# A four-layer kernel: the scan's C operand on VectorE, group norms by tiles, and group products placed later

## The chip, the cores and the metric

The kernel runs on one core of a Trainium2 chip. A core has engines that run side by side, each with an instruction queue of its own: TensorE (PE, matrix products, with its loading of weights shown as PEld), VectorE (DVE), ScalarE (ACT), GpSimd (POOL) and SyncE (SP, which here only issues DMAs). An engine takes its instructions in order; where one needs a result of another engine it waits on a semaphore, and all behind it in that queue waits too. DMAs are issued from the queues of SP, ScalarE and GpSimd. Matrix products land in PSUM; operands and results of the rest lie in SBUF.

The metric is device time in microseconds (us) of one execution, the median of several. A profile is one more execution, recorded by the hardware.

## The reference, cut to what matters

The input is x of (1, 1024, 64, 64), float32: 1024 channels by 4096 positions. Four layers follow, each as `x = x + f(norm(x))`, where the norm is a group norm over 32 groups of 32 channels:

```python
x = x + _L0_conv_ref(_gn(x), ...)   # layer norm and a decaying running sum along the channels
x = x + _L1_conv_ref(_gn(x), ...)   # 1024 x 1024 matrix on the channels, bias
x = x + _L2_conv_ref(_gn(x), ...)   # gated selective scan, below
x = x + _L3_conv_ref(_gn(x), ...)   # 1024 x 1024 matrix on the channels, bias
```

Layer 2, cut:

```python
xz = silu(einsum('oc,bchw->bohw', in_proj_w, x) + in_proj_b)     # 3072 x 1024
x_ssm, res, gate = split(xz, 3)
xf = silu(conv1d(x_ssm, dw_w) + dw_b)                            # along the tokens, width 3
dt, B_t, C_t = parts of einsum('oc,bcn->bon', dbc_w, xf)         # 2 heads, 8 states
# x_h, dt, B_t and C_t are put in a permuted order of the tokens, by head
h = exp(dt * A) * h + dt * B_t * x_t;  y_t = einsum(h, C_t)      # scan over 4096 tokens
# y is put back into the order of the tokens
y = y * silu(gate) + res
return silu(einsum('oc,bcn->bon', out_proj_w, y) + out_proj_b)
```

The group norm needs mean and variance of a whole group, so a layer's norm can't be finished until the layer before it has written the last position of the group's channels.

## The kernel before

**Tiles.** The 1024 channels are 8 tiles of 128 rows (`CT`), the 4096 positions are 8 blocks of 512 (`NB`), taken in pairs. Matrices: `W1` of layer 1, `WX`, `WR`, `WG` (the three thirds of the input projection: scan input, res and gate), `WO` (output projection) and `W3` of layer 3.

**Products in one step.** `W1`, `WX` and `WR` are multiplied by a Strassen-like scheme with seven products instead of eight (`multiply`, L813). For a pair of blocks the operand is cut in quarters: rows are channel tiles 0 to 3 and 4 to 7 (`KH` is 4 tiles), columns are the two blocks. `b_sets` (L773) makes the operands: `b21`, `b11`, `b22` by filling (ScalarE normalizes a tile of x, `normed`, L907 to L912), `t1` to `t4` by differences on VectorE or GpSimd. An output group `g` of two has two tiles of each row half, so group 0 writes channel tiles 0, 1, 4, 5 and group 1 writes 2, 3, 6, 7. A product is 8 calls of matmul with 512 columns (L828; the hardware runs each as two passes): for each of two output tiles `o`, the four tiles `k`. Its weights, 512 KB, come by a DMA on SP's queue. Results are added on VectorE (`put` and `add`). `run` (L867) goes over pairs and matrices, yields after every product, and (with `fine`) also after its first half.

**Order.** Instructions of VectorE, TensorE, GpSimd and ScalarE run in the order in which the program is written (`tc.manual_schedule`); SP's queue is ordered by the framework. Beside the products other work is dealt out: `sort_on` works on the ranking that gives the permutation, and `sum_weights` and `sum_weights2` make sums of weight blocks on GpSimd (L457 and after) and store them for later products.

**Norms.** While a layer's result is added up, VectorE takes statistics for every tile and block (`take_stats`, L148). `moments` (L176) aggregates them to mean and variance for each of the 8 tiles (L180), and `norm_steps` (L186) brings them to groups: a matmul over the group `pg` (L194), differences `d` (L197 to L199), a second matmul `pv` (L203), `v` (L211), Ln and Exp on ScalarE (L168, L169), a refinement (L171 to L173), and the bias (L214). Layer 2's norm is made in one piece (`norm2 = group_norm("gn2")`, L959) between the last product of layer 1 and the first of `WX`.

**The scan.** It runs beside the products of `WR`. Its 74 steps take 56 tokens of each of 2 heads. `gather` (L1212) fetches permuted rows, `turn_rows` (L1226, L1227) transposes them on TensorE into PSUM (`pr`), and `spread_decay` (L1230) makes from that the operands of the next step: `cts` and `bts` are copies of C and B (L1234, L1235), GpSimd makes `cd` from `cts` (L1236: C times an 8 by 8 identity, spread to 16 x 512), and VectorE makes `D` (L1239, L1241) and spreads it over the states into `E` (L1243). `cross` multiplies `bts` and `cd` on TensorE (`pg`, L1250); `weigh` on VectorE multiplies E by pg (L1258), reduces (L1260) and writes `G` (L1263); `apply` is the product `py` of G and the gathered rows (L1267). In one turn k of the loop: turn rows k+1, weigh k-1, spread k+1, products of `WR`, apply k-1, cross k. Results of `WR` go by `put2b` and `add2b` (L976, L980) into `rg`, and `activate` (L983) applies Silu (L986) and stores four tiles to DRAM (`res_d`) on SP's queue (L988). After the last step a loop (`while silus`, L1320) stores what is left.

**Products in two steps.** `WG`, `WO` and `W3` are multiplied with the scheme applied twice (`two_steps`, L1350): outer products P1 to P7, each of seven inner ones; a product "P7P3" is inner P3 of outer P7. A pair of blocks and a matrix make a job: first a gate job and an out job in turn for each pair, then last jobs (layer 3). Each inner product has a slot, and work is put at slots (`at`, `then`, `plan`): `fetch` (L1379) loads quarters of x (1 MB each) on ScalarE's queue, `fill` (L1386) normalizes them, `inner_sum` (L1384) makes differences on GpSimd, and `emit` (L1578) adds results out of PSUM, the first by ScalarE's copy (`qZ`, `qQ`, L1589). A row half of layer 3's norm is made by `next_norm` (L1429) during the last products of the out jobs: it begins at slot 44 or 56 of the job, goes on at +2, +2, +3, +3, and ends at +4.

Of the kernel before, what the change touches and what calls it, by code (L numbers as in the profile page):

```python
# [45 lines left out]
OG = 2  # L46
# [44 lines left out]
def tile_net(ctx: ExitStack, tc: tile.TileContext, x, par_d, cst_d, w_d, w2_d, dbcw_d, out):  # L91
# [84 lines left out]
    def moments(name, ct0=0, n=CT):  # L176

        mv = small.tile([P, 2, CT], F32, tag="gn_mv", name=f"{name}_mv")
        for ct in range(n):
            nc.vector.bn_aggr(mv[:, :, ct], stats[:, ct0 + ct].rearrange("p a b -> p (a b)"))  # L180
        return mv[:, 0, :n], mv[:, 1, :n]

    def group_norm(name):
        return finish_of(norm_steps(name, *moments(name)))
# [310 lines left out]
    with tc.issue_after(exp_ln.ins), tc.tile_pool(name="l0x", bufs=2) as lx, \  # L495
# [46 lines left out]
        def norm_chunk(c):  # L542

            at = slice(c * CH, (c + 1) * CH)
            mean, var = moments(f"gn0_{c}", c * CH, CH)
            nc.vector.tensor_copy(mean0[:, at], mean)
            nc.vector.tensor_scalar_mul(nmean0[:, at], mean, -1.0)
            norms[c] = yield from norm_steps(f"gn0_{c}", mean, var, CH, layernorm=True)
# [224 lines left out]
    def b_sets(B, make, first=False, eng=None):  # L773

        def plain(name, row, col):
            B[name] = []
            for k in range(KH):
# [35 lines left out]
    def multiply(m, B, put, add, fine=False):  # L813


        for g in range(NG):
# [7 lines left out]
            def product(to, i, name, fresh):  # L824
                w = weights(m, g, i)
                for o in range(OG):
                    for k in range(KH):
                        nc.tensor.matmul(to[o], w[:, k, o * P : (o + 1) * P], B[name][k],  # L828
                                         start=(fresh and k == 0), stop=(k == KH - 1),
                                         skip_group_check=True)  # L830
                    if fine and o == 0:
                        yield True
# [34 lines left out]
    def run(pairs, mats, make, put, add, before=None, after=None, last_eng=None, fine=False, tell=False, B=None):  # L867
# [3 lines left out]
        def sets(i):  # L871
            B = {"name": f"{mats[0]}_{pairs[i]}"}
# [9 lines left out]
        if B is None:  # L882
            B, steps = sets(0)
            for _ in range(5):
                next(steps)
        else:
            steps = iter(())
        for i, pair in enumerate(pairs):
# [3 lines left out]
            for m in mats:  # L892
                for half in multiply(m, B, lambda o, c, ps: put(m, o, 2 * pair + c, ps),
                                     lambda o, c, ps: add(m, o, 2 * pair + c, ps), fine):
                    if half:
                        yield True
                        continue
# [9 lines left out]
    def normed(norm):  # L907
        scale, bias = norm

        def make(t, ct, nb, eng=[0]):  # L910
            sc, bi = scale[:, ct : ct + 1], bias[:, ct : ct + 1]
            nc.scalar.activation(t, X[nb][:, ct, :], AF.Identity, bias=bi, scale=sc)  # L912
# [3 lines left out]
    def pointwise(name, m, bias_name, order, src, dst):  # L916
        norm = finish_of(norm_steps(f"gn{name}", mean1, var1))
# [31 lines left out]
    coming[0] = next(order)  # L949
    sums = (busy for f in (sum_weights(WR, sum1, nc.scalar, lag=(1, 1)),  # L950
                               sum_weights2(WG, sum1, nc.scalar, lag=(1, 1))) for busy in f)
    with tc.manual_schedule(engines={E_.DVE, E_.PE, E_.Pool, E_.Activation}):
        for i, _ in enumerate(pointwise("l1", W1, "b1", [3, 2] + EARLY, x0_d, x1_d)):
            busy = next(sums, None) if i % 14 < 13 else None
            sort_on(not busy, (0, 0, 0, 0, 3, 2, 1, 2, 1, 3, 3, 3, 0, 0)[i % 14])
        for _ in sums:
            pass
    sum_pool.__exit__(None, None, None)


    norm2 = group_norm("gn2")
# [21 lines left out]
    def activate(n):  # L983
# [3 lines left out]
        for o, nb, r in silus[:n]:  # L987
            nc.sync.dma_start(res_d[o * P : (o + 1) * P, nb * FB : (nb + 1) * FB], r)  # L988
        del silus[:n]

    with tc.tile_pool(name="l2a", bufs=2) as pa, tc.tile_pool(name="l2a2", bufs=1) as pa2, \
# [158 lines left out]
        with tc.manual_schedule(engines={E_.DVE, E_.PE, E_.Pool, E_.Activation}):  # L1150
# [4 lines left out]
            for half in run(EARLY + LATE, [WX], normed(norm2), put2a, add2a, before2,  # L1155
                            last_eng=nc.vector, fine=True, tell=True):
# [41 lines left out]
    with tc.tile_pool(name="l2r2", bufs=8) as prg, tc.tile_pool(name="l2g", bufs=5) as pgat, tc.tile_pool(name="l2b", bufs=2) as pb, tc.tile_pool(name="l2h", bufs=1) as ph, \  # L1198
# [31 lines left out]
        def spread_decay(k, R, BC, D):  # L1230

            bts, cd = B2[k % 2]
            cts = pb.tile([HS, LC], F32, tag="cts", name=f"cts{k}")
            nc.vector.tensor_copy(cts, BC[64 + 2 * HS : 64 + 3 * HS, P:])  # L1234
            nc.vector.tensor_copy(bts[:HS], BC[64 : 64 + HS, :P])  # L1235
            nc.gpsimd.tensor_tensor(cd[:HS], cts.unsqueeze(1).to_broadcast([HS, S, LC]),  # L1236
                                    eye8.unsqueeze(2).to_broadcast([HS, S, LC]), ALU.mult)
# [6 lines left out]
                                    negA.unsqueeze(2).to_broadcast([P, S, LC]), ALU.mult)  # L1244

# [41 lines left out]
        with tc.manual_schedule(engines={E_.DVE, E_.PE, E_.Pool, E_.Activation}):  # L1287
# [32 lines left out]
            while silus:  # L1320
                activate(4)
# [27 lines left out]
    def two_steps(jobs, norm2):  # L1349
# [5 lines left out]
        scale, bias = norm2  # L1355
# [390 lines left out]
```

## Time and profile before

| | us |
|---|---|
| median of 3 executions | 2760.11 (2759.61 to 2762.84) |
| profiled execution | 2760.86 |
| span of the profile in it | 2759.0 |
| TensorE busy | 2619.3 |
| VectorE busy | 1777.6 |
| ScalarE busy | 1090.0 |
| GpSimd busy | 1303.5 |

The span is what the profile covers, from the first instruction to the last; 1.86 us of the profiled execution lie around it. Busy times overlap. The mean clock granted to TensorE was 0.980 of full speed.

The program goes through these stretches, with TensorE's busy time in each as the profile's windows give it:

| stretch, us | TensorE busy | what runs |
|---|---|---|
| 0 to 300 | 221.72 | layer 0, start of layer 1 |
| 300 to 800 | 492.91 | layer 1 (to 615), then WX |
| 800 to 1400 | 584.28 | WX and convolution, then WR with the scan |
| 1400 to 1860 | 446.56 | WR with the scan (to 1673), then the gate and out jobs |
| 1860 to 2400 | 528.09 | gate and out jobs |
| 2400 to 2759 | 345.75 | layer 3 |

In lines of the timeline the columns are the start in us, the duration in us, the engine, the line, the operation, output and inputs by the program's names, shapes, how many instructions are taken together, and in brackets how long the engine had been idle and what it waited for. `SPq`, `ACTq` and `POOLq` are DMA issues and waits in an engine's queue. In a list of waits the columns are the time waited in all, how often, and the longest.

### The profile page before, as it was taken

The numbers are of one execution on the slowest core, as the hardware profiler recorded it, in microseconds if no ns is written. First come the engines' busy times: TensorE is split into PE (matmuls) and PEld (weight loads), VectorE is DVE, ScalarE is ACT, GpSimd is POOL, SyncE is SP. The second block draws the span as 40 slices with busy tenths as digits, with TensorE's granted clock in tenths as the row PEclk, the third lists the DMA queues.
The fourth block names the chain that finished last, engine by engine and source line by source line (L and its number), as shares of the span: only waits on it lengthen the run. The fifth ranks groups of instructions, "written<-read, shape, count | busy, mean of one in ns | idle before, by whom it ended". The sixth has DMA issues, their size and how long they took to land.

```text
span 2759.0 us, 31019 instructions
## 1 busy us (share of the span) xinstructions
PE 2619.3 (95%) x9590; PEld 1728.2 (63%) x9590; DVE 1777.6 (64%) x3785; ACT 1090.0 (40%) x1838; POOL 1303.5 (47%) x1175
## 2 busy tenths in 40 slices
PE   4788999999999999999999999999999999899998
PEld 4664444444555555444444446888888888788887
DVE  7996766464454564456666565567676675777776
ACT  4783110104655654565657554322333233221220
POOL 4154324411213002467686864556566575554543
PEclk9898999999999999999999999999999999999999
DMA  7345467745533534677777875889899898788896
GB/s 283 120 163 182 164 215 251 232 130 182 166 110 99 155 112 110 187 236 223 208 200 224 240 207 176 239 246 301 218 274 280 243 298 236 246 280 304 293 332 211
DMA packets 423578, 591.47 MB, mean 214 GB/s; under 512 B 149973, under 2 KB 211541, under 8 KB 420342
## 3 DMA queue, kind: packets, MB, share of 16 engines
q1 hardware_dynamic: 297110, 362.09, 42.2%
q10 hardware_dynamic: 93568, 140.52, 14.5%
q0 software_dynamic: 32736, 86.88, 12.2%
q8 instruction: 78, 1.28, 0.2%
q14 instruction: 86, 0.70, 0.1%
HBM read 432.02 MB, written 157.36 MB: 214 GB/s over the span
## 4 chain that ended last, share of the span: by engine, by line
PE 50%; DMA 3%; POOL 3%; DVE 3%; issue 1%; ACT 1%; DVEq 0%; POOLq 0%; ACTq 0%
PE mm L828 10%; PE q_P7P L1620 5%; PE q_P5P L1620 5%; PE q_P3P L1620 5%; PE q_P6P L1620 5%; PE q_P4P L1620 5%; PE q_P1P L1620 4%; PE q_P2P L1620 4%; PE pg L1250 2%; PE py L1267 2%; DMA qD<-x_d 2%; DMA g<-tok_d,src 1%; POOL s L457 1%; PE pr L1226 1%; POOL t L786 0%
## 5 line engine op out<-in xcount | busy, mean ns | idle before, releaser
L828 PE MATMUL mm<-t,w 128*128 128x512 f32 x1536 | 686.1, 598 | 0.3 <-DVE image L926 0.3
L828 PE MATMUL mm<-b,w 128*128 128x512 f32 x1152 | 518.4, 602 | 4.8 <-ACT b L912 4.8
L828 PEld LDWEIGHTS mm<-t,w 128*128 128x128 f32 x1536 | 287.6, 191 | 329.2 <-issue 324.1
L828 PEld LDWEIGHTS mm<-b,w 128*128 128x128 f32 x1152 | 218.0, 193 | 257.6 <-issue 246.8
L1017 DVE SCALAR_TENSOR_TENSOR cvp<-xs,par,cvp 128x512 f32<-128x512 f32 x128 | 95.4, 754 | 84.2 <-ACT cvp L1014 81.9
L1044 POOL TENSOR_TENSOR acc<-l2xt,acc 128x136 f32<-128x136 f32 x56 | 27.9, 498 | 246.6 <-ACT l2xt L1038 243.3
L1589 ACT COPY qQ<-q_P5P 128x512 f32<-128x512 f32 x48 | 28.1, 586 | 287.8 <-PE q_P5P L1620 256.0
L1388 ACT ACTIVATE qb<-x_x_b,gn_bias,gn_r_r 128x512 f32<-128x512 f32 x128 | 97.1, 805 | 112.6 <-DVE qQ L1550 49.2
L457 POOL TENSOR_TENSOR s<-s 128x256 f32<-128x256 f32 (+3 forms) x120 | 128.9, 1081 | 7.8
L1276 POOL DMA_INDIRECT y_d<-y,dst x74 | 75.4, 1019 | 118.0 <-ACT y L1272 55.5
L1270 ACT COPY g<-py 8x512 f32<-8x512 f32 x146 | 83.8, 574 | 108.9 <-PE py L1267 105.4
L1258 DVE TENSOR_TENSOR E<-E,pg 128x512 f32<-128x512 f32 x74 | 50.8, 686 | 109.9 <-PE pg L1250 101.9
L786 POOL TENSOR_TENSOR t<-b,t 128x512 f32<-128x512 f32 x72 | 94.4, 1339 | 55.1 <-DVE t L786 54.9
L926 DVE SCALAR_TENSOR_TENSOR image<-mm,par,image 128x512 f32<-128x512 f32 x64 | 47.2, 746 | 107.1 <-PE mm L828 107.1
L1068 DVE TENSOR_TENSOR xs<-mm,xs 128x512 f32<-128x512 f32 x64 | 41.7, 684 | 114.7 <-PE mm L828 114.7
L1036 PEld LDWEIGHTS l2pt<-both,cv 128*128 128x128 f32 x512 | 76.6, 190 | 35.6 <-issue 25.6
L1620 PE MATMUL q_P1P<-t_b,wq_P1P 128*128 128x256 f32 x384 | 93.6, 388 | 3.5 <-issue 3.5
L1384 POOL TENSOR_TENSOR t_t<-qt 128x512 f32<-128x512 f32 x23 | 29.7, 1289 | 139.8 <-DVE qt L1384 80.3
L1384 POOL TENSOR_TENSOR t_t<-qt,t_t 128x512 f32<-128x512 f32 x46 | 69.8, 1518 | 51.3 <-DVE qt L1384 51.0
L1620 PE MATMUL q_P4P<-t_t,wq_P4P 128*128 128x256 f32 x384 | 91.1, 380 | 0.0
L912 ACT ACTIVATE b<-image,gnl_bias,gnl_r_r 128x512 f32<-128x512 f32 x48 | 36.8, 808 | 137.4 <-DMA s<-in_w_dram 58.5
L1620 PE MATMUL q_P5P<-t_t,wq_P5P 128*128 128x256 f32 x384 | 90.8, 379 | 0.0
(381 smaller groups left out, 5999.6 us busy)
## 6 DMA issues: line engine op xcount, KB each, us to landing
w<-s_d SPq DMA_DIRECT2D x96, 512.0 KB
w<-in_w_dram SPq DMA_DIRECT2D x72, 512.0 KB
x_x_b<-x_d ACTq DMA_DIRECT2D x32, 1024.0 KB
image<-x_d SPq DMA_DIRECT2D x12, 2048.0 KB
wq_P6P<-s_d SPq DMA_DIRECT2D x84, 256.0 KB
wq_P7P<-s_d SPq DMA_DIRECT2D x84, 256.0 KB
wq_P5P<-s_d SPq DMA_DIRECT2D x84, 256.0 KB
wq_P3P<-s_d SPq DMA_DIRECT2D x84, 256.0 KB
```

What stands on the lines that cost most here:

```text
L457: eng.tensor_tensor(out, a, b, ALU.subtract)
L786: eng.tensor_tensor(B[name][k], B[one][k], B[two][k], ALU.subtract)
L828: nc.tensor.matmul(to[o], w[:, k, o * P : (o + 1) * P], B[name][k], start=(fresh and k == 0), stop=(k == KH - 1), skip_group_check=True)
L1017: nc.vector.scalar_tensor_tensor(cv, xo[:, at + t : at + t + FB], pcol("dww", 3 * o + t), cv, ALU.mult, ALU.add)
L1036: nc.tensor.matmul(pt[:, q * NV : (q + 1) * NV], cv[:, (q0 + q) * P : (q0 + q + 1) * P], both[:, o, :], start=True, stop=True)
L1250: nc.tensor.matmul(pg, bts, cd.rearrange("p s t -> p (s t)"), start=True, stop=True)
L1267: nc.tensor.matmul(py, G2[k % 2], rows.pop(k)[:, :DH], start=True, stop=True)
L1270: nc.scalar.copy(rows[k + 1][h * LC : h * LC + S, :DH], py[h * LC : h * LC + S])
L1276: nc.gpsimd.indirect_dma_start(out=y_d[:, :], out_offset=bass.IndirectOffsetOnAxis(ap=dst_[:, k : k + 1], axis=0), in_=y[:, :], in_offset= ...
L1384: eng.tensor_tensor(to, a, b, ALU.subtract)
L1388: nc.scalar.activation(tile_of(j, name)[:, k], held[j, "x", name][:, k], AF.Identity, bias=bias[:, k : k + 1], scale=scale[:, k : k + 1])
L1620: nc.tensor.matmul(ps[:, o, :], w[:, k, o * P : (o + 1) * P], rhs[:, k, :], start=(new and o == 0 and k == 0), stop=(k == 1), skip_group_c ...
```

## The change

It has five parts.

1. **C's operand.** `cts` and GpSimd's product `cd` are taken away; one VectorE instruction behind the spread of E reads C from PSUM and writes `cd`.
2. **Layer 2's norm by tiles.** The tiles of group 0 (`FIRST`) are aggregated after the first of layer 1's last seven products, and their norm `gn2a` is made in steps after the products that follow. The others (`SECOND`) are aggregated half after the last but one product, half later; their norm `gn2b` is written after the first half of the first product of `WX`. That product (`b21`) is split: first the tiles k = 0, 1 for both output tiles, then k = 2, 3. Before its first half only the fills of k = 0, 1 stand.
3. **Layer 3's norm.** The steps of a row half stand at slots +3, +3, +4, +4 instead of +2, +2, +3, +3; its end at +4 for the first half and at +5 for the second. The fill of `b21` of the first last job begins at slot 12 instead of 11.
4. **Queues.** The stores of res in the last loop go on GpSimd's queue instead of SP's. Loads of x for the first job go on SP's queue instead of ScalarE's; the order of SP's queue then has them early in the scan, and the two stores ahead of GpSimd's first differences of the gate job.
5. **Bookkeeping.** Norms are kept by channel tile (`columns`), without an instruction of its own.

```diff
+    def moments(name, tiles, some=None, mv=None):
+        if mv is None:
+            mv = small.tile([P, 2, CT], F32, tag="gn_mv", name=f"{name}_mv")
+        for i in range(len(tiles)) if some is None else some:
+            nc.vector.bn_aggr(mv[:, :, i], stats[:, tiles[i]].rearrange("p a b -> p (a b)"))
+        n = len(tiles)
+        return mv if some is not None else (mv[:, 0, :n], mv[:, 1, :n])
...
                 w = weights(m, g, i)
-                for o in range(OG):
-                    for k in range(KH):
-                        nc.tensor.matmul(to[o], w[:, k, o * P : (o + 1) * P], B[name][k],
...
-                    if fine and o == 0:
+                split = begun and g == 0 and i == 1
+                for j in range(2):
+                    for o, ks in ((0, range(2 * j, 2 * j + 2)), (1, range(2 * j, 2 * j + 2))) if split else ((j, range(KH)),):
+                        for k in ks:
+                            nc.tensor.matmul(to[o], w[:, k, o * P : (o + 1) * P], B[name][k],
...
+                    if fine and j == 0:
                         yield True
...
             for _ in range(5):
-                next(steps)
+            for _ in range(5 if begun is None else 0):
+                next(steps)
...
                     if half:
                         yield True
+                        if B is begun and "b11" not in B:
+                            for _ in range(5):
+                                next(late)
                         continue
...
+    norm2, last = {}, NP * NG * 7 - 1
+    FIRST, SECOND = ([row * KH + g * OG + o for row in range(2) for o in range(OG)] for g in range(NG))
...
+            if i == last - 6:
+                chain = norm_steps("gn2a", *moments("gn2a", FIRST), len(FIRST), finer=True)
+            elif last - 6 < i < last - 1:
+                next(chain)
+            elif i == last - 1:
+                columns(FIRST, finish_of(chain), norm2)
+                mv2 = moments("gn2b", SECOND, range(2))
...
+        begun = {"name": f"{WX}_{EARLY[0]}", "b21": [b_tile("b21", k, f"{WX}_{EARLY[0]}") for k in range(2)]}
+        for k in range(2):
+            normed(norm2)(begun["b21"][k], KH + k, 2 * EARLY[0])
-    norm2 = group_norm("gn2")
...
+                if len(norm2) < CT:
+                    moments("gn2b", SECOND, range(2, 4), mv2)
+                    n = len(SECOND)
+                    columns(SECOND, finish_of(norm_steps("gn2b", mv2[:, 0, :n], mv2[:, 1, :n], n)), norm2)
...
-    def activate(n):
+    def activate(n, dma=nc.sync):
...
-            nc.sync.dma_start(res_d[o * P : (o + 1) * P, nb * FB : (nb + 1) * FB], r)
+            dma.dma_start(res_d[o * P : (o + 1) * P, nb * FB : (nb + 1) * FB], r)
...
-            cts = pb.tile([HS, LC], F32, tag="cts", name=f"cts{k}")
-            nc.vector.tensor_copy(cts, BC[64 + 2 * HS : 64 + 3 * HS, P:])
             nc.vector.tensor_copy(bts[:HS], BC[64 : 64 + HS, :P])
-            nc.gpsimd.tensor_tensor(cd[:HS], cts.unsqueeze(1).to_broadcast([HS, S, LC]),
-                                    eye8.unsqueeze(2).to_broadcast([HS, S, LC]), ALU.mult)
...
             nc.vector.tensor_tensor(E, D.unsqueeze(1).to_broadcast([P, S, LC]),
                                     negA.unsqueeze(2).to_broadcast([P, S, LC]), ALU.mult)
+            nc.vector.tensor_tensor(cd[:HS], BC[64 + 2 * HS : 64 + 3 * HS, P:].unsqueeze(1).to_broadcast([HS, S, LC]),
+                                    eye8.unsqueeze(2).to_broadcast([HS, S, LC]), ALU.mult)
...
             while silus:
-                activate(4)
+                activate(4, nc.gpsimd)
...
-            nc.scalar.dma_start(t, rows_of(d, row, 2 * pair + col))
+            (nc.scalar if key[0] else nc.sync).dma_start(t, rows_of(d, row, 2 * pair + col))
...
-            for row, slot in ((0, 44), (1, 56)):
+            for row, slot, after, last in ((0, 44, (3, 3, 4, 4), 4), (1, 56, (3, 3, 4, 4), 5)):
...
-                for i in (2, 2, 3, 3):
+                for i in after:
                     then(s0 + slot + i, go_on)
-                then(s0 + slot + 4, end)
+                then(s0 + slot + last, end)
...
-                        (("b11", 0, 0, -7, -1), ("b12", 0, 1, -3, 2), ("b21", 1, 0, 3, 11), ("b22", 1, 1, 8, 14))
+                        (("b11", 0, 0, -7, -1), ("b12", 0, 1, -3, 2), ("b21", 1, 0, 3, 12), ("b22", 1, 1, 8, 14))
```

## The prediction

> **What bounds the kernel now.** I read the page's engine totals first, then TensorE's waits, and then the timeline around each wait that the diff touches.
>
> ```profile
> PE 2619.3 (95%) x9590; PEld 1728.2 (63%) x9590; DVE 1777.6 (64%) x3785; ACT 1090.0 (40%) x1838; POOL 1303.5 (47%) x1175
> ```
>
> TensorE is busy for 2619.3 of 2759.0 us, so the end moves only by what TensorE's idle time of 139.7 us and its slow stretches lose. The windows put some 78 us of that idle time ahead of 300 us (142.80 busy of 215, 78.92 of 85), where the change does nothing. The waits name the rest (columns: us in total, times, longest):
>
> ```profile
> PE gn_pg L194 <- DVE gn_mv L180: 42.1, 7, 22.5
> PE pg L1250 <- POOL cd L1236: 9.8, 7, 2.3
> ...
> PE py L1267 <- DVE G L1263: 7.1, 6, 2.6
> ...
> PE q_P1P L1620 <- ACT qb L1388: 6.2, 3, 2.3
> ...
> PE mm L828 <- ACT b L912: 4.8, 2, 2.4
> ...
> PE q_P1P L1620 <- issue: 3.5, 1, 3.5
> ```
>
> Of the 42.1 us, the change can reach the three waits at layer 2's and layer 3's norms (2.0, 4.7, 2.4 in the timeline). So at most about 35 us are in reach, plus clock losses behind the gaps.
>
> **Part 1, C's operand in the scan.** Per step it removes VectorE's copy (L1234, 0.225 us) and GpSimd's product (L1236, 1.033 us), and adds one VectorE product of 16x512 reading PSUM, behind the spread of E. Its nearest row is that spread (L1243, 128x512, PSUM in, 0.691 us). Over 74 steps GpSimd loses 76.4 us and VectorE gains 74 x (0.691 - 0.225) = 34.5 us. One step's timeline:
>
> ```profile
> 1225.11 2.21 POOL L457 TENSOR_TENSOR s<-s 128x256 f32<-128x256 f32 x3
> ...
> 1225.29 0.69 DVE L1243 TENSOR_TENSOR E<-pr,negA 128x512 f32<-128x512 f32 x1
> ...
> 1227.28 1.03 POOL L1236 TENSOR_TENSOR cd<-cts,cst 16x512 f32<-16x512 f32 x1
> ...
> 1228.37 1.12 PE L1250 MATMUL pg<-cd,bts 66*128 66x512 f32 x2 [1.90 <-POOL cd L1236]
> ```
>
> GpSimd does three additions of the weight sums before cd, and TensorE waits 1.90 us. In the new order cd ends on VectorE near 1225.29 - 0.22 + 0.69 + 0.69 = 1226.45, when TensorE has just finished py: the wait goes. So I take all seven away: **-9.8**.
>
> Behind this gap stands a second loss, in the windows (PE, PEld, DVE, ACT, POOL busy, then the granted clock):
>
> ```profile
> 1230.00:1232.00 2.00, 2.00 (x4) 0.97 (x4) 1.89 (x5) 0.00 (x0) 1.92 (x2) 0.50 0.68 182
> 1232.00:1234.00 2.00, 2.00 (x4) 0.72 (x4) 1.67 (x6) 0.35 (x1) 1.90 (x2) 0.70 0.82 217
> ```
>
> At 0.50 and 0.70 these lose 1.0 and 0.6 us of work. [...] The trace shows half clock after 1.90 us, but none after gaps of 2.03 us at 1210 and 1.84 at 1428: a gap is punished now and then. Behind cd's gaps I find this twice: here, and in the window 1580 to 1600 (0.91 of 20 us, 1.8 lost). I take the row: **-3.4**.
>
> What hides VectorE's extra 0.47 us a step is its idle time before it weighs E (L1258): 101.9 us in 58 of 74 steps, waiting for TensorE's pg. In the other 16, behind the new product are E's weighing, G, and TensorE's py that reads G. In six of these py already waits for G (the 7.1 us), so 6 x 0.47 = **+2.8**; in the rest G is ready 0.84 us or more before py. Sum: -9.8 - 3.4 + 2.8 = **-10.4**, between -6 (half the clock losses return behind longer G waits) and -13 (G's waits don't grow).
>
> **Part 2, layer 2's norm.** Before, the whole chain stood open between the last product of layer 1 and the first of layer 2:
>
> ```profile
> 614.83 0.59 PE L828 MATMUL mm<-t,w 128*128 128x512 f32 x1
> ...
> 617.43 0.36 PE L194 MATMUL gn_pg<-gn_mv,cst 128*128 128x8 f32 x2 [2.01 <-DVE gn_mv L180]
> ...
> 618.54 0.36 PE L203 MATMUL gn_pv<-gn_d,cst 128*128 128x8 f32 x2 [0.75 <-DVE gn_d L199]
> ...
> 620.42 1.52 ACT L912 ACTIVATE b<-image,gn_bias,gn_r_r 128x512 f32<-128x512 f32 x2 [0.84 <-DVE gn_bias L214]
> 621.28 0.28 PEld L828 LDWEIGHTS mm<-b,w 128*128 128x128 f32 x1 [2.48 <-ACT b L912]
> ```
>
> Now half of the tiles have their norm during the last seven products of layer 1. ScalarE can fill two tiles of b21 once it has issued the stores of x (1.00 us from 616.18), and TensorE starts near 618.1 with half the product: 8 passes of 0.43 us, to 621.5. But the second half's pg stands in TensorE's queue **behind** these 8 passes, though its operand is there at 617.3. From pg to the first matmul the old chain took 621.28 - 617.43 = 3.85 us, and it is still whole: 621.5 + 3.85 = 625.4, and 8 more passes end at 628.8. Before, the product ended at about 630.5, part of it at clock 0.50 and 0.59. [...] The first half's pg and pv, four small matmuls in the last products, cost 0.3 to 0.4. Ends -1.4 and +1.4; I take **0**, since before's clock did fall here.
>
> **Part 3, last stores of res and first loads of the gate job.** Between the scan and the gate product:
>
> ```profile
> 1669.23 5.93 SPq L988 DMA_DIRECT2D res_d<-rg  x5
> ...
> 1674.10 0.93 ACTq L1381 DMA_DIRECT2D x_x_b<-x_d  x2
> ...
> 1681.24 2.22 ACT L1388 ACTIVATE qb<-x_x_b,gn_bias,gn_r_r 128x512 f32<-128x512 f32 x3 [3.60 <-DMA res_d<-rg]
> ...
> 1684.07 0.56 ACT L1589 COPY qZ<-q_P1P 128x512 f32<-128x512 f32 x1
> ...
> 1684.73 1.62 PE L1620 MATMUL q_P1P<-t_b,wq_P1P 128*128 128x256 f32 x3 [3.48 <-issue]
> ```
>
> TensorE's 3.48 us come from ScalarE: it waits 3.60 us for a buffer that a res store has still to leave, fills it, and only then copies qZ out of PSUM. That store shares the DMA engines with two 1 MB loads of x issued at the same moment. In the change the x loads go on SP's queue, where they stand near 1500 us, so they have long landed; the two stores go on GpSimd's queue at about 1673 and 1675.5. Without the competitors I put the store's landing at 1678.5 instead of 1681.2 and the gap 2.7 us shorter. The passes behind it run at 0.67 (window 1680 to 1690) and took 6.58 us for 16 where 3.46 is warm: up to 3.1 more. Ends: 0 (the store lands no earlier from GpSimd's queue) and -5.8; I take **-4**. Moved with these: behind the loads on SP stand weight loads of the scan, 3 MB more ahead of them, some 10 us at the 300 GB/s that windows here show. The DMA share there is 0.68 to 1.03; the weights are loaded products ahead, so I count nothing. On GpSimd the stores stand ahead of the combination t1, which waits for one of them already (76.4 us of its work are gone besides).
>
> **Part 4, layer 3's norm.** pg of its first half now stands behind product P7P3, and pv behind P4P7.
>
> ```profile
> 2392.25 0.59 PE L194 MATMUL gn_pg<-gn_mv,cst 128*128 128x4 f32 x2 [4.73 <-DVE gn_mv L180]
> ```
>
> P7P3 (1.73 us warm) moves into the 4.73 us before it. After it came P7P3 at 3.76 us, P4P7 at 2.27, with the clock at 0.50 to 0.58, and a gap of 2.29 before P1P1 at 2401.09. New: pg still at 2392.25, P4P7 covers d, pv at about 2395.8, the bias 2.0 us later, P1P1 near 2398.7: -2.4 (-1.9 when cold). The second half waits 2.41 before pg; a product of 1.7 fills it, but 0.5 and 0.75 come back at pv and at P2P1: about -0.4. Sum **-2.6**, between -1 and -4.
>
> **The sum**: -10.4 + 0 - 4 - 2.6 = -17.0. The span of 2759.0 becomes 2742; 1.86 us lie around it (2760.86 measured), and the median of before, 2760.11, is 0.75 below its profiled run: 2742 + 1.86 - 0.75 = **2743**.
>
> **Rivals.**
> - *Only the waits for GpSimd go*: clock losses merely move, part 3 gains nothing, the norms return what they save: -9.8 + 2.8 and a little = -8, 2752. For it: the punishment by the clock is erratic, and the store in part 3 may be slow by itself. Against: P7P3 is in the open gap for certain. Chance 0.24.
> - *Everything pays*: -13 - 1.4 - 5.8 - 4 = -24, 2736. For it: each gap removed stands before a cold stretch. Against: pg behind the half product. Chance 0.24.
> - *VectorE becomes the bound of the scan*, slower: if the 0.47 us were exposed in all 74 steps, +34.5 against -13.2 (waits and clock) and -6.6 (parts 3 and 4) gives +14.7, 2775. It decides where VectorE's idle time before E falls under 0.47 us in more than about 42 steps (19.8 / 0.47); the trace has 16 such steps, and G's slack above 0.84 in ten of them. A late weight load on SP behind the 3 MB would have the same sign. Chance 0.03.
> - *The change doesn't do what it says*: cd is late on VectorE too, because VectorE reaches E's spread late; the waits carry VectorE's name and nothing is won: 2758, no change. Chance 0.03.
>
> **The numbers.** The forecast has 0.46. About 0.2% (5.5 us) is what a measurement of this kernel tells from no change. Faster 0.94, within 0.03, slower 0.03. The range reaches to both neighbours: 2734 to 2753.
>
> **What would show it.** TensorE's wait for cd gone from its list, VectorE's total near 1812 (1777.6 + 34.5), GpSimd's near 1227; py's wait for G near 10 us; the new product at 0.69 us. In part 2 a wait of 2 to 3 us before the second half of the first product; in part 3 the 3.48 us under 1; in part 4 the wait before pg at 3.0. Wrong it would be if the new product took over 1 us, if waits for weights appear after 1500, or if the clock falls in new places.

## The result, and the profile after

The changed kernel took 2752.92 us (median of 8, 2746.57 to 2756.69) beside 2763.07 us before (median of 8, 2757.86 to 2764.86). The ratio is 0.9966, with a 95% interval of 0.9955 to 0.9977: 9.4 us gained of 2760, where 17 were forecast. The profiled execution took 2756.69 us, the longest of the eight; its span is 2754.8.

The engine totals of the page after:

```profile
PE 2622.8 (95%) x9594; PEld 1731.6 (63%) x9594; DVE 1818.7 (66%) x3793; ACT 1090.1 (40%) x1840; POOL 1225.4 (44%) x1103
```

VectorE gained 41 us and GpSimd lost 78. The first part of the change alone (`b_cd` below) brings 34.3 and 78.1. TensorE's waits after (us in all, times, longest):

```profile
PE gn_pg L198 <- DVE gn_mv L181: 36.1, 6, 22.6
...
PE py L1290 <- DVE G L1286: 9.1, 6, 3.7
...
PE mm L835 <- ACT b L921: 7.4, 3, 2.7
...
PE pr L1251 <- DMA g<-tok_d,src: 6.0, 5, 2.4
...
PE q_P1P L1641 <- ACT qb L1409: 5.5, 3, 2.7
...
PE q_P1P L1641 <- POOL t_b L1405: 1.5, 1, 1.5
```

The wait for cd (9.8 us) is gone. In its place stands one that the list of before does not have: `pr`, the transposing of the gathered rows, waits 6.0 us for the gather's DMA. The wait of the first products of a layer for ScalarE's fill (`mm` for `b`) is longer, 7.4 us after 4.8. And where ScalarE's late copy cost 3.48 us at the gate job, 1.5 are left.

To see where the time went I compared the start of the same instruction in both traces, and cut the program in stretches at such instructions: from the ninth last sum of L930 into the image (L940 in the changed kernel) to ScalarE's ninth copy into xs (the turn from layer 1 to 2); from the first weighing of E to the last sum into rg (the scan); from there to the second P6P sum into qZ (the turn to the gate job); from there to a sum of P4P ahead of layer 3's norm (gate and out jobs); from there to the fourth P3P sum behind it (layer 3's norm). All lengths are in us. The runs are those of the next section.

| run | 1 to 2 | scan | to gate | jobs | norm 3 | ratio to before (95%) |
|---|---|---|---|---|---|---|
| before | 106.60 | 536.06 | 36.11 | 591.69 | 191.89 | 1 |
| after | 109.87 | 530.80 | 29.55 | 595.04 | 191.34 | 0.9966 (0.9955 to 0.9977) |
| b_cd | 106.61 | 524.24 | 35.11 | 595.73 | 193.98 | 0.9961 (0.9948 to 0.9973) |
| a_fetch_act | 111.17 | 524.40 | 35.31 | 598.42 | 190.93 | 0.9973 (0.9963 to 0.9983) |
| a_gn2_early | 102.93 | 533.78 | 29.55 | 593.25 | 190.33 | 0.9945 (0.9928 to 0.9961) |
| a_gather_first | 106.75 | 540.31 | 29.74 | 595.17 | 191.33 | 0.9993 (0.9979 to 1.0006) |
| a_x_late | 109.56 | 525.79 | 29.51 | 593.77 | 191.33 | 0.9956 (0.9939 to 0.9972) |
| c_early_late | 102.78 | 525.46 | 29.52 | 593.45 | 190.92 | 0.9928 (0.9912 to 0.9945) |
| a_warm | 106.75 | 530.33 | 29.55 | 595.13 | 189.36 | 0.9968 (0.9957 to 0.9980) |
| a_gn3_old | 106.75 | 529.50 | 29.55 | 593.13 | 193.77 | 0.9986 (0.9977 to 0.9994) |
| a_stores_sp | 109.45 | 527.47 | 29.55 | 596.17 | 190.31 | 0.9966 (0.9958 to 0.9974) |
| c_gather5 | 103.41 | 519.67 | 29.50 | 594.96 | 190.78 | 0.9923 (0.9910 to 0.9937) |
| c_warm | 102.84 | 525.04 | 29.52 | 591.32 | 189.36 | 0.9942 (0.9929 to 0.9956) |

One row is one profiled execution. How far chance moves a stretch is seen in the jobs, which no run changes: 591.32 to 598.42, with before's own profile near the low end. Before and after differ by only 4.2 us in their profiles and by 9.4 in their times; 3.4 of these 5.2 us lie in the jobs.

### The profile page after: what moved, and what is told of

The parts are those of the page before. It is cut to its first block, busy times and chain, and to the rows that moved or that the text cites. A ratio compares the mean times of both kernels' runs of the same rounds, so it can differ in the third digit from the quotient of the medians.

```text
span 2754.8 us, 30917 instructions
## 1 busy us (share of the span) xinstructions
PE 2622.8 (95%) x9594; PEld 1731.6 (63%) x9594; DVE 1818.7 (66%) x3793; ACT 1090.1 (40%) x1840; POOL 1225.4 (44%) x1103
## 3 DMA queue, kind: packets, MB, share of 16 engines
q0 software_dynamic: 32896, 87.40, 12.4%
## 4 chain that ended last, share of the span: by engine, by line
PE 44%; POOL 5%; DMA 5%; issue 3%; DVE 2%; ACT 1%; SPq 0%; POOLq 0%; DVEq 0%; ACTq 0%
PE mm L835 8%; PE q_P6P L1641 5%; PE q_P3P L1641 5%; PE q_P7P L1641 5%; PE q_P2P L1641 4%; PE q_P5P L1641 4%; PE q_P4P L1641 4%; PE q_P1P L1641 4%; DMA y_d<-y,dst 2%; DMA qD<-x_d 2%; POOL s L461 1%; PE py L1290 1%; PE pg L1273 1%; DMA g<-tok_d,src 1%; POOL t_b L1405 1%
## 5 line engine op out<-in xcount | busy, mean ns | idle before, releaser
L1409 ACT ACTIVATE qb<-x_x_b,gn_bias,gn_r_r 128x512 f32<-128x512 f32 x64 | 48.9, 806 | 113.0 <-DMA wq_P4P<-s_d 32.3
L1641 PE MATMUL q_P2P<-t_b,wq_P2P 128*128 128x256 f32 x384 | 92.0, 383 | 0.0
```

The lines of the kernel that those rows point to most:

```text
L1409: nc.scalar.activation(tile_of(j, name)[:, k], held[j, "x", name][:, k], AF.Identity, bias=bias, scale=scale)
L1641: nc.tensor.matmul(ps[:, o, :], w[:, k, o * P : (o + 1) * P], rhs[:, k, :], start=(new and o == 0 and k == 0), stop=(k == 1), skip_group_c ...
```

## The experiments

### The first part alone, and the x loads back on ScalarE's queue

The scan gained 5.3 us where the prediction had 10.4. Two theories: the gathers were always late and cd's wait had hidden it (A), or the x loads that now stand in SP's queue make them late (B). `b_cd` is the kernel before with the first part alone; `a_fetch_act` is the changed kernel with

```diff
-            (nc.scalar if key[0] else nc.sync).dma_start(t, rows_of(d, row, 2 * pair + col))
+            nc.scalar.dma_start(t, rows_of(d, row, 2 * pair + col))
```

> The kernel before with part 1 alone (VectorE makes C's operand from PSUM). Theory A, the gathers of the permuted rows are late by themselves (they stand behind scatters in GpSimd's queue) and their wait takes the place of the one removed: TensorE's wait for cd is 0, its wait for gathered rows 4 to 7 us (0 before), the scan is about 5 us shorter, the time about 4 us under before. Theory B, the gathers of the changed kernel are late because of the x loads that part 3 put into SP's queue: the wait for gathered rows is under 1 us here, the scan 8 to 10 us shorter, the time 8 to 10 us under before. In both VectorE gains 34 us of busy time.

> The changed kernel with the x loads of the first gate job back on ScalarE's queue; the stores of res stay on GpSimd's. Theory A (late gathers by themselves): the wait for gathered rows stays at 4 to 7 us. Theory B (the x loads make them late): it is under 1 us and the scan some 5 us shorter. For the turn to the gate job: if the loads beside the stores are the cause of the late buffer, TensorE's gap before P1P6 goes from 1.5 us back to about 3.5 and the clock falls behind it, 4 to 6 us lost there; if the change of queue was enough, the gap stays at 1.5.

Both runs have the short scan, 524.24 and 524.40 us, 11.8 and 11.7 less than before. TensorE's waits between 1120 and 1670 us of `b_cd`:

```profile
PE py L1265 <- DVE G L1261: 7.7, 6, 2.3
PE pr L1226 <- DMA g<-tok_d,src: 3.7, 2, 1.9
```

The wait for cd is gone, that for G went from 7.1 to only 7.7 us, and 3.7 us of waiting for gathered rows have come in its place. So A holds for about 3.5 us (3.2 in `a_fetch_act`), and B for the rest. The part alone has ratio 0.9961: as much as the whole change.

The loss also lies where B puts it. I cut the scan at the fiftieth weighing, near 1485 us and ahead of the loads. The part behind it takes 183.5 us on average in the five traces that have the loads early and each gather behind its scatter (182.0 to 184.5), and 178.3 and 178.2 in these two; the part ahead of it takes 346.9 against 346.0 and 346.2. What the loads do in the changed kernel stands in SP's and GpSimd's queues and in TensorE's:

```profile
1525.48 2.12 SPq L1402 DMA_DIRECT2D x_x_b<-x_d  x2
...
1563.09 0.91 SPq L1632 DMA_DIRECT2D wq_P1P<-s_d  x2
...
1568.77 0.99 POOL L1299 DMA_INDIRECT y_d<-y,dst  x1 [7.77 <-issue]
...
1592.43 0.99 POOL L1299 DMA_INDIRECT y_d<-y,dst  x1 [4.42 <-DMA y_d<-y,dst]
...
1593.47 0.55 PE L1251 MATMUL pr<-cst,g 128*112 128x192 f32 x2 [1.90 <-DMA g<-tok_d,src]
```

Three x loads of 1 MB go out between 1525 and 1535 us, and push most of the gate job's weights, which `a_fetch_act` issues from 1509 us on, to 1563 to 1567. The DMA share of the window 1560 to 1580 is 0.86 here and 0.62 in `a_fetch_act`. Right behind it TensorE waits for rows at 1593 and again at 1602 (1.90 and 2.41 us; `a_fetch_act` has only one such wait there, of 1.69).

The gathers themselves are not slowed; the scatters ahead of them in GpSimd's queue are. Four traces that tell when gathers and scatters landed show it (that of after does not tell). The two scatters issued between 1550 and 1569 us around a gather take 6.4 us on average from issue to landing in `a_stores_sp` and `a_gn2_early`, which have the loads early, and 4.2 in `a_fetch_act` and `b_cd`; the gather between them takes 7.1 and 7.3 us in the first two, 7.3 and 6.5 in the others. In all four the second scatter begins 3.36 us behind the landing of the first. GpSimd idles 7.77 us ahead of it in the changed kernel, 5.60 in `a_fetch_act`, and the gathers behind it go out late: those of three steps in a row are issued 6.0, 7.2 and 6.4 us ahead of the turning of their rows, where `a_fetch_act` has 8.7, 9.9 and 7.2. Whether the x loads slow the scatters or the weights that they pushed back was not tried.

At the turn to the gate job `a_fetch_act` shows why the loads help from SP. Its timeline:

```profile
1668.82 0.93 ACTq L1402 DMA_DIRECT2D x_x_b<-x_d  x2
...
1676.55 1.52 ACT L1409 ACTIVATE qb<-x_x_b,gn2a_bias,gn2a_r_r 128x512 f32<-128x512 f32 x2 [4.20 <-DMA res_d<-rg]
...
1680.05 4.32 PE L1641 MATMUL q_P1P<-t_b,wq_P1P 128*128 128x256 f32 x12 [5.76 <-issue]
```

With the loads issued beside the stores, ScalarE waits 4.20 us for the buffer of a store and TensorE 5.76 us behind it, though the stores are on GpSimd's queue. That store, issued at 1669.84 us, takes 6.6 us to land; in `c_gather5` (below), with no load beside it, the same store takes 2.3. The changed kernel has 1.50 us at this place:

```profile
1680.39 3.69 PE L1641 MATMUL q_P1P<-t_b,wq_P1P 128*128 128x256 f32 x16 [1.50 <-POOL t_b L1405]
```

So the early loads cost the scan some 4 to 6 us and save the turn 6: moved with next to no net gain.

### The stores' queue

`a_stores_sp` is the changed kernel with the stores back on SP (`activate(4)`).

> The changed kernel with the last stores of res back on SP's queue; the x loads stay on SP's queue early in the scan. Theory: the turn to the gate job is short because the loads are there and no longer beside the stores, whichever queue the stores use: the stretch to the first P6P sum stays at 29.5 to 30.5 us (35.1 and 35.3 where the loads were issued beside the stores, from either queue of the stores). Rival: the queue of the stores is a part of it; the stretch is 2 to 4 us longer.

The turn stays at 29.55 us, the ratio at 0.9966. The queue of the stores does nothing here; the company of the loads was the cause (35.11 us in `b_cd` and 35.31 in `a_fetch_act` with it).

### The x loads held until the scan's DMAs are done

If the loads must neither meet the scan's gathers nor the last stores, there is a gap for them: in `a_fetch_act` the DMA share is 0.15 between 1640 and 1650 us and 0.07 between 1650 and 1660. `a_x_late` puts them behind the last store of weight sums:

```diff
+                last_sum[0] = dma.dma_start(s2_d[m][:, j, :, at].rearrange("i p e -> p i e"), v)
...
+            if key[0]:
+                nc.scalar.dma_start(t, rows_of(d, row, 2 * pair + col))
+            else:
+                with tc.issue_after(last_sum[0].ins):
+                    nc.sync.dma_start(t, rows_of(d, row, 2 * pair + col))
```

> The changed kernel with the x loads of the first gate job on SP's queue, but held until behind the last store of weight sums (near 1635 us; the DMA share between 1640 and 1660 was 0.15 and 0.07 in the run with the loads on ScalarE's queue). Theory B2, the loads cost the scan where they meet its gathers and weights, and help the gate job by being there: the scan is as short as with the loads on ScalarE's queue (some 524 us between its first and last weighing, 531 in the changed kernel) and the turn to the gate job as short as in the changed kernel (29.6 us to the first P6P sum, 35.3 with ScalarE's queue); 5 to 7 us under the changed kernel in all. Rival: what the scan lost had another cause (VectorE's added work, chance of the clock), the scan stays at 530 and the time within 2 us of the changed kernel.

SP's queue in this run:

```profile
1634.20 4.06 SPq L490 DMA_DIRECT2D s_d<-s  x4
1638.32 3.79 SPq L1408 DMA_DIRECT2D x_x_b<-x_d  x4
```

The scan is 525.79 us and the turn 29.51: both gains at once. The wait for gathered rows in it is 2.4 us. The ratio, 0.9956, is 2.8 us under the changed kernel's, where 5 to 7 were expected; the intervals overlap, so the stretches carry the verdict.

### Fills and group products of layer 2's norm earlier

The turn from layer 1 to 2 was to cost nothing more or less; it got longer. The changed kernel's timeline there:

```profile
603.42 0.41 PE L361 MATMUL sort<-cst,turned 128*64 128x128 f32 x2 [0.91 <-DVE gn2a_v L215]
...
618.33 1.00 ACTq L137 DMA_DIRECT2D x_d<-image  x2
...
619.38 1.52 ACT L921 ACTIVATE b<-image,gn2a_bias,gn2a_r_r 128x512 f32<-128x512 f32 x2 [15.14 <-DVE stats L148]
...
620.24 5.13 PE L835 MATMUL mm<-b,w 128*128 128x512 f32 x8 [2.68 <-ACT b L921]
...
625.21 0.28 PE L198 MATMUL gn2b_pg<-gn2b_mv,cst 128*128 128x4 f32 x2
...
628.88 6.68 PE L835 MATMUL mm<-b,w 128*128 128x512 f32 x11 [2.36 <-ACT b L921]
```

The norm of the first tiles was ready at 615.4, but its two fills stand behind the stores of x, which wait for the last sum; so they start at 619.38, 1.8 us behind layer 1's last product. And pg stands behind the half product. Ahead of all this, a product of the ranking waits 0.91 us for a step of the first norm on VectorE (603.42). `a_gn2_early` writes the two fills ahead of the last product, pg behind a quarter of the first product and pv behind three eighths:

```diff
             elif i == last - 1:
                 columns(FIRST, finish_of(chain), norm2)
                 mv2 = moments("gn2b", SECOND, range(2))
+                begun = {"name": f"{WX}_{EARLY[0]}", "b21": [b_tile("b21", k, f"{WX}_{EARLY[0]}") for k in range(2)]}
+                for k in range(2):
+                    normed(norm2)(begun["b21"][k], KH + k, 2 * EARLY[0])
...
+                            if split and j == 0:
+                                for _ in range(B["between"].get(2 * o + k, 0)):
+                                    next(B["chain"])
```

> The changed kernel with part 2 put otherwise: the two fills of b21 stand ahead of the stores of x in ScalarE's queue, the second half's pg behind a quarter of the first product, its pv behind three eighths. Theory E, the loss of part 2 is the place of these in the queues: the gap of 2.7 us before the first product goes, the one before its second half falls from 2.4 to about 1.5, the product ends 9.5 to 11 us after the last product of layer 1 (16.4 in the changed kernel), 5 to 7 us under the changed kernel at this place. Rival: ScalarE's fills for the next products are then late, or the clock falls all the same; under 3 us gained.

```profile
614.56 1.52 ACT L924 ACTIVATE b<-image,gn2a_bias,gn2a_r_r 128x512 f32<-128x512 f32 x2 [11.25 <-DVE gn2a_bias L218]
```

That line is from ScalarE's timeline; TensorE's is

```profile
616.48 1.88 PE L835 MATMUL mm<-b,w 128*128 128x512 f32 x4
618.75 0.35 PE L198 MATMUL gn2b_pg<-gn2b_mv,cst 128*128 128x4 f32 x2 [0.39 <-DVE gn2b_mv L181]
618.97 1.10 PE L835 MATMUL mm<-b,w 128*128 128x512 f32 x2
619.91 0.28 PE L207 MATMUL gn2b_pv<-gn2b_d,cst 128*128 128x4 f32 x2
620.05 1.10 PE L835 MATMUL mm<-b,w 128*128 128x512 f32 x2
622.55 5.85 PE L835 MATMUL mm<-b,w 128*128 128x512 f32 x13 [1.40 <-ACT b L924]
```

The fills are done before layer 1 ends, the first product follows without a gap, and 0.39 and 1.40 us are all that is waited. The turn takes 102.8 to 103.4 us in the four runs that have it so, 108.6 on average in the seven that have it as the change does (106.75 in three of them without half clock there, 109.5 to 109.9 in three with 6.83 us of it, 111.17 in one with 10.24), and 106.6 before, with 6.83 us of half clock. The ratio falls to 0.9945.

### The gather ahead of the scatter

In the changed kernel scatters wait for earlier ones at the head of GpSimd's queue (the 4.42 us above), and a gather stands behind each. `a_gather_first` swaps the two calls in the scan's loop.

> The changed kernel with the gather of a scan step issued ahead of the scatter of the step before it, which in GpSimd's queue can wait for earlier scatters to land. Theory A: the wait for gathered rows falls from 6.0 us to under 1, the scan is 4 to 6 us shorter than in the changed kernel. Rival: the rows are late in the DMA queue itself, not at its door: the wait stays at 4 to 7 us and the time is that of the changed kernel within 2 us.

Both theories fell: the wait for gathered rows rose to 10.9 us, and the scan took 540.31. GpSimd's waits between 1120 and 1680 us:

```profile
POOL y_d L1299 <- DMA y_d<-y,dst: 49.4, 14, 5.5
POOL s L481 <- DMA s_d<-s: 35.1, 13, 4.0
...
POOL g L1237 <- PE py L1290: 18.7, 11, 3.6
```

In the changed kernel the first two are 28.3 us and 11.0. Scatters and the stores of weight sums were later, and a gather that stands first stops GpSimd until py is done. Which of these made the rows late was not tried.

### Both together, and rows gathered a step earlier

`c_early_late` has the early fills and the held loads.

> The changed kernel with both: fills ahead of the stores and the second norm's group products inside the first half product (as in the run before), and the x loads held until 1635 us. If the two effects add: 5 to 7 us under the run with the first alone (2746 median there), ratio to before near 0.992. If they share a cause: no lower than 0.9945.

Turn, scan and gate are 102.78, 525.46 and 29.52: the effects add. The ratio is 0.9928, the median 2741.17, some 4.7 us under the run with the early fills alone. It still waits 4.4 us for gathered rows. `c_gather5` gathers five steps ahead, with six buffers for the rows (5 before) and seven for rg (8 before):

```diff
-                if 3 < k + 4 < NK:
-                    gather(k + 4)
+                if 4 < k + 5 < NK:
+                    gather(k + 5)
```

> The version of both (early fills, held x loads) with the rows of the scan gathered five steps ahead instead of four; room for the sixth buffer comes from one buffer of rg less (7). Theory A2, what is left of the wait for gathered rows is the time from issue to landing: 4.4 us of it go to under 1, and the scan is 3 to 6 us shorter than 525. Rival: the seventh buffer is missed, ScalarE's copies of WR's results wait for stores, TensorE waits for their banks; the scan gets longer.

Its list of TensorE's waits between 1100 and 1680 us has three lines and none for the rows; the first two:

```profile
PE py L1298 <- DVE G L1294: 9.1, 6, 3.7
PE q_P1P L1653 <- ACT qb L1421: 2.2, 1, 2.2
```

The scan is 519.67 us, 16.4 less than before. With a median of 2736.47 us and a ratio of 0.9923 (0.9910 to 0.9937) this version is well ahead of both kernels and has the lowest ratio of all. The interval overlaps that of `c_early_late`, so that here too the scan carries the verdict. TensorE's waits show no sign that the buffer of rg is missed.

### Layer 3's norm: the old slots, and a warm clock

In after's profile this stretch gained 0.55 us where 2.6 were forecast. `a_gn3_old` puts its steps (and the fill of b21) back.

> The changed kernel with part 4 undone (layer 3's norm at the slots of before). Theory: TensorE's waits at this place go back from 8.5 us to 12.2 and the stretch is 2 to 4 us longer at the same amount of half clock. Rival: the five sums of P7P3 that now stand ahead of the differences on VectorE take back what the moved product brings; the stretch is the same within 1 us.

The stretch is 193.77 us; TensorE idles 12.2 us in it, and 8.6 in after. The three traces with the old slots (before, `b_cd`, this) average 193.2 us, the eight with the new ones and no added products 190.9: the part brings 2.3 us. Half clock is the same in both groups, 9.1 and 9.4 us on average; the single pair before and after had hidden the gain behind it (6.83 and 13.65 us). In whole times undoing the part costs more, a ratio of 0.9986 (0.9977 to 0.9994) beside 0.9966, which is 5.5 us (the intervals touch at 0.9977); where the other 3 us come from stays open. The windows of after (TensorE's busy time first, granted clock third from the end):

```profile
2386.00:2390.00 4.00, 1.65 (x5) 1.47 (x6) 3.96 (x11) 0.00 (x0) 0.00 (x0) 0.73 1.01 352
2390.00:2394.00 4.00, 2.79 (x9) 2.16 (x7) 2.50 (x9) 0.41 (x2) 0.00 (x0) 0.50 1.00 333
2394.00:2398.00 4.00, 2.48 (x6) 1.99 (x7) 0.51 (x4) 1.52 (x2) 1.26 (x1) 0.50 0.17 60
2398.00:2402.00 4.00, 4.00 (x12) 3.03 (x10) 0.02 (x1) 2.65 (x4) 0.00 (x0) 0.56 0.28 66
```

Half clock for 13.65 us in a row, twice as long as before. `a_warm` fills the two gaps with products that nobody reads:

```diff
+        def keep_warm(calls):
+            for _ in range(calls):
+                nc.tensor.matmul(pg[:, 256:512], cst[:, CST["ident"]], cst[:, :256], start=True, stop=True,
+                                 skip_group_check=True)
+        keep_warm(warm[0])
...
+        keep_warm(warm[1])
```

There are six calls ahead of pg and four behind pv.

> The changed kernel with products that nobody reads in the two gaps of layer 3's first norm: six of 128x256 ahead of pg (2.6 us of the 2.99 us gap), four behind pv (1.7 of 2.73). Theory C, the half clock behind this norm (13.65 us of it in the changed kernel, 6.83 before) comes from TensorE's idle gaps: the half clock is gone or at most one stretch of 3.4 us, the products from P4P7 on run at full speed, 3 to 5 us less between the norm and the next sums. Rival: the clock falls for another reason (the DMA load, the narrow products): half clock and time as in the changed kernel within 1 us.

```profile
2384.00:2388.00 4.00, 2.42 (x12) 1.71 (x11) 3.93 (x12) 0.00 (x0) 0.00 (x0) 1.00 0.98 297
2388.00:2392.00 4.00, 2.89 (x13) 1.93 (x13) 1.22 (x6) 1.93 (x4) 0.00 (x0) 1.00 0.74 287
2392.00:2396.00 4.00, 3.27 (x14) 2.56 (x14) 0.00 (x0) 2.40 (x3) 1.26 (x1) 1.00 0.27 66
```

The clock stays at 1.00 in the gaps; one stretch of 3.41 us is left behind them, where after has 13.65. So the long half clock came here with the idle gaps. The gain is 2.0 us against after's profile and 1.5 against the average of the new slots, less than expected: TensorE still waits 0.41, 1.17 and 1.10 us there, for VectorE and for ScalarE's fill. In the ratio (0.9968) it can't be seen. `c_warm` adds the same products to `c_early_late`.

> The version of both with the unread products in the gaps of layer 3's first norm. If what the run with these products showed at this place carries over: the stretch around layer 3's norm is 189 to 190 us instead of 190.9, the time 1 to 2 us under 2741. If not: the same within 1 us.

The stretch is 189.36 us again. The median, 2740.25, and the ratio, 0.9942 (0.9929 to 0.9956), don't confirm a gain in all.

## Why the prediction was right and wrong

The parts are numbered as in the prediction; its parts 3 and 4 are the fourth and the third in the list of the change.

- **Part 1 in the scan: right in sum, not in its terms.** With the x loads out of the way it gains 11.8 us (10.4 forecast). The seven waits for cd are gone (9.8 us), and so are 6.83 us of half clock, the 3.4 us that were taken from the trace. But the six waits for G grew by 0.6 us, not 2.8 (by 2.0 in after, where one of them stands behind the difference of 2.04 us on VectorE told at the end), and 3.2 to 3.7 us of waiting for gathered rows came up behind cd, which the prediction does not have. So its three terms, measured, make -12.6 and the rows take some of it back; with a wait of 1.0 us for ScalarE's y that also went, the account of `b_cd` is -9.9, and 1.9 us stay open. The new product took 0.693 us, as its nearest row said.
- **Part 3, the step that failed.** The prediction saw 3 MB of x loads ahead of other work in SP's queue, asked only about the scan's own weights, and wrote "I count nothing". What slowed were the scatters, on another queue (6.4 us from issue to landing beside 4.2), and so the gathers behind them were issued late. Five traces with the loads early and the gather behind the scatter average 530.4 us for the scan; with the loads on ScalarE's queue it takes 524.3. That is a term of +6.1, of which 5.3 lie behind the fiftieth weighing. Of these, 1.0 does not go away when the loads are held: in the three traces that hold them and gather four steps ahead, that part takes 179.2 us and has the longer wait for G. The turn itself gained 6.0 (35.5 on average in the three traces with loads and stores together, 29.5 else), within the stated ends, where -4 was taken. So the part is worth next to nothing, where it was to bring 4.
- **Part 2: +2.0 for 0.** The chain behind layer 1's last product was right: 2.68 us to the first product, pg behind the half product, 2.36 us of wait before the second half. Both ends lie some 1.5 us too low: +0.15 and not -1.4 where the clock stays up, about +3 and not +1.4 where it falls. Of that, 0.91 us is the ranking's product that waits for the first norm on VectorE, a consumer in TensorE's queue that was not asked about. And the clock fell in four of seven traces, so that a value in the middle was too kind. No run shows the two ends between which the 0 was taken: beside 106.6 us before, the turn took 106.75 where the clock stays up, 109.5 to 109.9 with 6.83 us of half clock and 111.17 with 10.24.
- **Part 4: right, -2.3 for -2.6.** pg waits 2.99 us, as forecast at 3.0; that after's own profile shows only -0.55 fits the 6.8 us more of half clock in it.

Added up: -11.8 + 6.1 - 6.0 + 2.0 - 2.3 = -12.0 us, against a measured 9.4 with an interval of 6.3 to 12.4. Of the 5 us between the forecast and this sum, the uncounted 6.1 is the largest term; the 2.6 us between the sum and the measured time lie inside the interval and are not accounted for.

## What to carry to other kernels

When a load is moved to where "its queue has time", look at which transfers of other queues run in that stretch, and at what waits for them to land before it may issue the next (here the scatters, 6.4 us to landing beside 4.2); give it the stretch in which the DMA share is low (here 0.15 and 0.07). Held to 1638 us, the same four loads kept both gains. When a wait is removed, find what stands just behind it; here it was the rows gathered four steps ahead, and a fifth step made the scan 5.8 us shorter. And a first half made early pays only if its consumers, and the next stage's small products, stand ahead of whatever waits for the end: here the turn took 102.8 to 103.4 us so, and 108.6 on average otherwise.

## What the runs showed of the hardware

**Of TensorE's gaps of 1.5 to 3 us, some stood beside half clock and some did not.** Over the thirteen traces, behind 300 us, I counted TensorE's idle gaps and those with a stretch of half clock beginning from 4 us before to 3.5 us behind their end: 9 of 180 gaps of 0.2 to 1.5 us, 10 of 44 of 1.5 to 2, 50 of 78 of 2 to 2.5, 15 of 26 of 2.5 to 3, and all 35 above 3; in before and after alone 1 of 27, 15 of 29 from 1.5 to 3, and all 5. One gap, of 2.45 us in both, ahead of P6P in the out jobs, shows it; in TensorE's timeline of before and of after it stands as

```profile
2064.42 1.56 PE L1620 MATMUL q_P6P<-qt,wq_P6P 128*128 128x256 f32 x6 [2.45 <-DVE qt L1384]
```

```profile
2056.88 2.93 PE L1641 MATMUL q_P6P<-qt,wq_P6P 128*128 128x256 f32 x6 [2.45 <-DVE qt L1405]
```

and the six products behind it take 1.56 us in one and 2.93 in the other. The pieces of half clock last 3.41 us or multiples of it (13.65 is four), but for the last of each trace (5.57 us before, 3.85 after).

The traces of before and after show where the two differ. Their 14 and 15 pieces of half clock begin on a grid of 3.413 us, one for each trace, that they meet within 0.01 us. A grid point cuts before's gap of 2.45 us in 0.67 and 1.78: TensorE idles 0.67 us of the grid window from 2059.22 us and 1.78 of the next, and the clock stays at 1.00. In after 2.34 us of the gap lie in the one window from 2053.35, and the clock is 0.50 in the window behind it. So the grid lies differently against the program in the two traces, 0.67 and 2.34 us behind the start of the same gap. I take this for chance, and for the likeliest reason that single profiles differ by some microseconds in stretches that no edit touches (591.32 to 598.42 us for the jobs); neither was shown.

**VectorE's operations on two SBUF tiles took longer beside GpSimd's.** Operations on two SBUF tiles (128x512) on VectorE never took over 0.694 us in after's trace while no elementwise operation of GpSimd ran beside them (171 of them); of 156 that met one, 116 took over 1 us, up to 2.85. Where one of the two operands came from PSUM, none took over 0.693 us, though 506 met one. In the timeline of VectorE in after, and in `a_fetch_act`, four differences of two SBUF tiles:

```profile
1510.52 3.84 DVE L790 TENSOR_TENSOR t<-t,b 128x512 f32<-128x512 f32 x4
```

```profile
1511.89 2.49 DVE L790 TENSOR_TENSOR t<-t,b 128x512 f32<-128x512 f32 x4
```

In the first, GpSimd's additions begin 0.3 us behind the fourth, which takes 2.04 us; in the second they begin after it. The 1.35 us between the two come back as TensorE's wait for G, 3.68 us instead of 2.36. The traces do not show by what one engine holds up the other.
